# First attention of a perceiver block: the key and value projection split over four steps, its row tiles moved behind p * v, its evictions in every second step

## The chip, the cores and the metric

The kernel runs on one core of one Trainium2 chip. The metric is the device time of one execution in microseconds (us); several executions of the same kernel are listed and their median is used. All data are f32.

## The reference

The program is six residual blocks in a row, on 128 queries of width 256. The change is in the first one, a cross attention from the queries to a context of 12544 rows of width 192, with 16 heads of width 16:

```python
x = x + L0_xattn(layernorm(x), ctx)      # the changed part
x = x + L0_attn(layernorm(x)); x = x + L0_ffn(layernorm(x))
x = x + L1_xattn(layernorm(x), ctx); x = x + L1_attn(layernorm(x)); x = x + L1_ffn(layernorm(x))

def L0_xattn(x, y):                      # y: 12544 x 192
    q = x @ Wq + bq; k = y @ Wk + bk; v = y @ Wv + bv       # 16 heads of 16
    attn = softmax(q k^T / sqrt(16))                        # per head, 128 x 12544
    out = attn v
    return relu(out @ W1 + b1) @ W2 + b2
```

## The kernel before, in words

The first attention goes over the context twice, for eight heads (an octet, 128 columns of k and v) at a time. The context is cut into superblocks of 1024 rows; a pass has twelve full ones and a last one of 256 rows. Each superblock gives four groups of 256 rows (the last one gives one), so there are 98 groups in all.

One step t of the loop issues, by hand (the order is written out, nothing reorders it), on each engine's queue:

- TensorE (PE): the scores of group t (L428, eight matmuls as four row tiles of 32), at times the transposes for a range maximum, then the pieces of the projection for group t + 4 (AHEAD = 4), then p * v of group t - 13 (LAG = 13; L530, in four column tiles of 32), then at times more transposes. Where the flag `same` is true, the pieces of the projection come behind p * v instead of ahead of it.
- ScalarE (ACT): two copies of the scores from PSUM to SBUF (L441), then two exponents of group t - 12 (L517).
- VectorE (DVE): two running maxima over the scores (L447; they read the same PSUM tiles as the two copies, in the other order), one part of the shift by the maximum (L506), then the evictions of the projection from PSUM: keys with bias (L390), values (L256).
- GpSimd (POOL): the larger part of the shift by the maximum for group t - 12 (L506).

The scores of a step take two PSUM tiles of two banks each, and there are only these: the scores of step t + 1 use the banks of step t. The projection and the small transposes share two banks with the tag "w"; two more banks are single ("m", "o").

The projection of one superblock is made of a key unit and a value unit. A unit has *row tiles* (`tiled`, the 64 rest rows of the 192, for both halves r of the superblock at once, in row tiles of 64; L209 for keys, L227 for values) and two *whole* parts (`whole(r)`, the 128 main rows for one half; L212, L234), then one eviction for each half (`keys_out`, `values_out`). With g the number of a group in its superblock, the pieces in step t are those of group t + 4: g = 0 key row tiles, whole(0) and eviction 0; g = 1 key whole(1) and eviction 1; g = 2 and 3 the same for the values. An *even* step below is one whose pieces have g 0 or 2, an *odd* step one with g 1 or 3.

Groups are taken in ranges of ten (or nine), each with its own maximum. The first step of a range, called step +0 here, also folds the maximum of the range before it (L464 or L462, DVE), transposes it on PE (L474) and reduces it on DVE (L475). Step +1 spreads it out with transposes on PE (L250) and two copies on ACT (L494). A range's p * v ends two steps after the next range but one has begun: in step +2 its result is copied (L540), in step +3 turned by two transposes on PE into a "w" bank (`gather`, L245) and stored (L546). In the second pass one such gather falls on step +4.

While t is under 12, the evictions are on ACT, after that on DVE. In the steps up to 13 there is no p * v.

Of the kernel before, what the change touches and what calls it, by code (L numbers as in the profile page):

```python
# [13 lines left out]
P = 128  # L14
# [19 lines left out]
def perceiver(ctx: ExitStack, tc: tile.TileContext, a: dict, out: bass.AP):  # L34
    nc = tc.nc
# [5 lines left out]
    banks = {}  # L41
# [34 lines left out]
    def context_weight(pool, name, ap):  # L76
# [18 lines left out]
        out=headmask, in_=headmask, compare_op=ALU.is_ge, fill=0.0, base=0,  # L95
# [3 lines left out]
        out=headmask, in_=headmask, compare_op=ALU.is_ge, fill=0.0, base=15,  # L99
# [4 lines left out]
    for u in range(2):  # L104
# [6 lines left out]
        out=causal, in_=causal, compare_op=ALU.is_ge, fill=-1e10, base=0,  # L111
# [71 lines left out]
    NS = (SK + SB - 1) // SB  # L183
# [32 lines left out]
    def project_values(name, wv, cx, j, bank=None):  # L216

        lo, hi, h = cx
        ps = [(bank or ps_w)(f"{name}_{r}") for r in range(2)]
        js = slice(j * P, (j + 1) * P)  # L220

        def tiled():
            for kc in range(h // P):
                ks = slice(kc * P, (kc + 1) * P)
                for r in range(2):
                    rs = slice(64 * r, 64 * r + 64)
                    nc.tensor.matmul(  # L227
                        ps[r][:, ks], hi[rs, ks], wv[1][rs, js], start=(kc == 0), stop=False,
                        skip_group_check=True,
                    )  # L230

        def whole(r):
            for kc in range(h // P):
                nc.tensor.matmul(  # L234
                    ps[r][:, kc * P : (kc + 1) * P], lo[:, r * h + kc * P : r * h + (kc + 1) * P],
                    wv[0][:, js], start=False, stop=True, skip_group_check=True,
                )

        return ps, tiled, whole
# [59 lines left out]
    with tc.tile_pool(name="l0w", bufs=1) as lw:  # L299
# [8 lines left out]
        with tc.tile_pool(name="l0x", bufs=1) as work, ExitStack() as ps0:  # L308
# [51 lines left out]
            def spare(name):  # L360

                return bank_o(name) if name.endswith("_1") else bank_m(name)

            def behind(t):

                return ((1, 2), (3, 4), (5, 6), (7,))[t] if t < 4 else (t + AHEAD,)

            def pieces(t):

                if t >= len(groups):  # L370
                    return []
# [8 lines left out]
                work_of = {"k": ([], [], []), "v": ([], [], [])}  # L380
# [16 lines left out]
                def first_half(kind, make, w, evacuate):  # L397
                    bank = spare if kind == "v" and m < 2 else None
                    unit = make(f"x0_{kind}{m}", w, ctxs[m], j, bank)
                    tiled, whole, out = work_of[kind]  # L400
                    tiled.append(unit[1])
                    whole.append(lambda: unit[2](0))
                    out.append(lambda: evacuate(0, unit[0][0]))
                    deferred[m, kind] = lambda: unit[2](1), lambda: evacuate(1, unit[0][1])
# [5 lines left out]
                short = s == NS - 1  # L410
                if g == 0:
                    first_half("k", project_keys, xwk, keys_out)
                if g == 1 or short:
                    second_half("k")
                if g == 2 or short:
                    first_half("v", project_values, xwv, values_out)
                if g == 3 or short:
                    second_half("v")
                return [f for kind in "kv" for part in work_of[kind] for f in part]

            def scores(t):
                m, g = groups[t]
# [126 lines left out]
                )  # L549

            with tc.manual_schedule():
                tiled, whole, k_out = pieces(0)
                tiled()
                whole()
                early = ps_s("x0_early")
                _, xnT = layernorm(x, "ln0", early[:, 0])
                k_out()
                queries(0, xnT, early[:, 1])
                oTs = {}

                spread_at = {max(l + 2, l0 + LAG - 2): b for b, (l0, l) in enumerate(zip(start_of, last_of))}
                for t in range(len(groups) + LAG + 1):
                    e, o = t - LAG + 1, t - LAG
                    e = e if 0 <= e < len(groups) else None
                    o = o if 0 <= o < len(groups) else None
                    st = scores(t) if t < len(groups) else None
                    ended = range_of[t - 1] if 1 <= t < len(groups) + 1 and last[t - 1] else None
                    b = spread_at.get(t)
                    spread = range_spread(b) if b is not None else None
                    if e is not None:  # L570
                        shifted_gpsimd(e)
                        if first[e]:
                            shifted_vector(e)
# [739 lines left out]
```

## Time and profile before

| | us |
|---|---|
| median of 3 runs | 1596.38 |
| lowest, highest | 1593.13, 1598.63 |
| the profiled execution's own time | 1592.66 |
| its span | 1590.9 |
| first scores of the first attention start at | 13.86 |
| step +1 of its last but one range: spread maximum copied, by | 402.3 |
| last exponents of the first attention end at about | 456 |

The granted clock of TensorE was 0.987 of full speed over the span and 1.00 in the stretch from 0 to 440 us. A profile comes from one execution; its rows give, for groups of equal instructions, the count, the busy time, the mean duration of one, and the idle time of the engine ahead of them with the instruction that ended it. A timeline row gives the start, the length, the engine, the line and the operation, and in brackets the idle time ahead and what ended it. Each f32 matmul shows as two records of it. A chain of waits tells which instruction each one waited for last.

### The profile page before, as it was taken

To read this page: it belongs to the slowest core of one execution; us is meant where nothing else is said; L and a number is where in the kernel's file an instruction comes from. 1 tells how busy PE (TensorE), PEld (TensorE's weight loads), DVE (VectorE), ACT (ScalarE), POOL (GpSimd) and SP (SyncE) were. 2 spreads that over 40 slices of the span, in tenths; PEclk is the share of its full clock that TensorE was granted. 3 is DMA by queue.
4 is the path that set the end of the run, shared out by engine and by line. 5 is a ranking of instruction groups with operands and counts; after the bars stand their busy time and mean duration, and the time that the engine had idled before them with its cause. 6 is when DMAs were issued, how large, how long until landed. Compare 5 with 4: busy or idle time off the path is not lost.

```text
span 1590.9 us, 39751 instructions
## 1 busy us (share of the span) xinstructions
PE 1507.9 (95%) x17130; PEld 1156.8 (73%) x17130; DVE 1169.4 (74%) x1238; ACT 996.3 (63%) x1221; POOL 851.1 (54%) x559
## 2 busy tenths in 40 slices
PE   7999989999789998999999999999999999999978
PEld 4566666666545877877778787787787777777868
DVE  4798978999863327677777777777777777778952
ACT  5898979889853225665655665565665655655531
POOL 0588877888820000863863864864764764761000
PEclk9999999999997999999999999999999999999979
DMA  3211112111193661322222222232232222225930
GB/s 104 61 41 42 46 42 61 41 42 46 47 270 129 238 167 25 98 84 83 83 80 86 81 81 86 80 93 74 87 94 80 87 81 86 81 81 153 306 135 4
DMA packets 68737, 146.62 MB, mean 92 GB/s; under 512 B 8905, under 2 KB 27089, under 8 KB 68562
## 3 DMA queue, kind: packets, MB, share of 16 engines
q1 hardware_dynamic: 68258, 143.30, 30.0%
q8 instruction: 135, 2.21, 0.6%
q10 hardware_dynamic: 304, 0.79, 0.2%
q14 instruction: 40, 0.33, 0.1%
HBM read 143.92 MB, written 0.13 MB: 91 GB/s over the span
## 4 chain that ended last, share of the span: by engine, by line
PE 62%; DVE 6%; ACT 2%; POOL 1%; DMA 1%; issue 1%; SPq 0%; DVEq 0%; ACTq 0%
PE x_s L958 11%; PE x_v L234 10%; PE x_o L1043 10%; PE x_k L212 9%; PE x_v L227 5%; PE x_k L209 4%; PE f_h L1249 2%; PE f_h L824 2%; PE k L212 2%; PE f_py L841 2%; DVE x_part L1066 1%; POOL x_p L506 1%; PE k L209 1%; DVE x_folded L1005 1%; PE f_py L1258 1%
## 5 line engine op out<-in xcount | busy, mean ns | idle before, releaser
L1024 POOL TENSOR_TENSOR x_p<-x_p,x_spread 128x1024 f32<-128x1024 f32 (+1 forms) x175 | 402.6, 2324 | 165.1 <-ACT x_spread L1017 164.9
L506 POOL TENSOR_TENSOR x_p<-x_p,x_spread 128x512 f32<-128x512 f32 (+1 forms) x184 | 325.6, 1820 | 121.0 <-ACT x_spread L494 61.1
L1066 DVE TENSOR_REDUCE x_part<-x_p 128x256 f32<-128x1024 f32 (+1 forms) x175 | 329.4, 1923 | 1.6 <-ACT x_p L1032 1.6
L975 ACT COPY x_p<-x_s 128x1024 f32<-128x1024 f32 (+1 forms) x200 | 198.0, 996 | 177.7 <-DVE x_mx L982 97.9
L982 DVE TENSOR_TENSOR x_mx<-x_s,x_mx 128x1024 f32<-128x1024 f32 (+1 forms) x161 | 193.4, 1201 | 127.1 <-PE x_s L958 118.7
L1071 POOL TENSOR_TENSOR x_sums<-x_sums,x_part 128x256 f32<-128x256 f32 x161 | 118.7, 738 | 303.4 <-DVE x_part L1066 303.1
L441 ACT COPY x_p<-x_s 128x1024 f32<-128x1024 f32 x196 | 193.4, 1016 | 48.5 <-PE x_s L428 33.2
L234 PEld LDWEIGHTS x_v<-ywv_lo,x_ctx_lo 128*128 128x128 f32 x1568 | 189.3, 192 | 38.3 <-issue 36.8
L1032 ACT ACTIVATE x_p<-x_p 128x1024 f32<-128x1024 f32 (+1 forms) x200 | 197.8, 1037 | 1.4 <-DVE x_p L1024 1.3
L517 ACT ACTIVATE x_p<-x_p 128x1024 f32<-128x1024 f32 x196 | 196.3, 1062 | 0.2 <-DVE x_p L506 0.2
L1043 PE MATMUL x_o<-x_p,x_v 128*64 128x128 f32 x3136 | 193.6, 276 | 0.4
L234 PE MATMUL x_v<-ywv_lo,x_ctx_lo 128*128 128x128 f32 x1568 | 193.1, 276 | 0.0
L447 DVE TENSOR_TENSOR x_mx<-x_s,x_mx 128x1024 f32<-128x1024 f32 x140 | 168.2, 1221 | 32.1 <-PE x_s L428 17.2
L1043 PEld LDWEIGHTS x_o<-x_p,x_v 128*64 128x64 f32 x3136 | 169.6, 137 | 12.3 <-issue 1.5
L958 PE MATMUL x_s<-x_qT,x_kT 64*128 64x128 f32 x2744 | 177.7, 279 | 0.0
L212 PE MATMUL x_k<-x_ctx_lo,ywk_lo 128*128 128x512 f32 (+1 forms) x364 | 171.6, 594 | 0.0
L958 PEld LDWEIGHTS x_s<-x_qT,x_kT 64*128 64x128 f32 x2744 | 160.2, 188 | 15.6 <-issue 15.4
L943 ACT COPY x_v<-x_v 128x512 f32<-128x512 f32 (+1 forms) x208 | 116.2, 563 | 79.3 <-PE x_v L234 78.8
L227 PEld LDWEIGHTS x_v<-ywv_hi,x_ctx_hi 64*128 64x128 f32 x1568 | 106.8, 188 | 48.4 <-issue 25.1
L428 PE MATMUL x_s<-x_qz,x_kT 32*128 32x256 f32 x1568 | 117.6, 401 | 17.7 <-ACT x_p L441 16.6
L530 PE MATMUL x_o<-x_p,x_v 128*32 128x128 f32 x3136 | 111.7, 276 | 10.0 <-ACT x_p L517 8.5
L530 PEld LDWEIGHTS x_o<-x_p,x_v 128*32 128x32 f32 x3136 | 81.9, 109 | 53.9 <-ACT x_p L517 18.9
(257 smaller groups left out, 1761.1 us busy)
## 6 DMA issues: line engine op xcount, KB each, us to landing
x_ctx_lo<-in_ctxT_dram SPq DMA_DIRECT2D x119, 512.0 KB, 4.0
x_ctx_hi<-in_ctxT_dram SPq DMA_DIRECT2D x238, 128.0 KB, 3.8
f_w<-in_L_ffn_W_dram SPq DMA_DIRECT2D x32, 512.0 KB, 4.9
k_lo<-in_ctxT_dram SPq DMA_DIRECT2D x12, 512.0 KB, 10.0
f_gating<-n_kernel_gating_EDF_dram SPq DMA_DIRECT2D x8, 512.0 KB, 6.9
f_up<-L_ffn_kernel_up_EDF_dram SPq DMA_DIRECT2D x8, 512.0 KB, 7.5
f_wd<-ffn_kernel_down_EFD_dram SPq DMA_DIRECT2D x8, 512.0 KB, 7.3
k_hi<-in_ctxT_dram SPq DMA_DIRECT2D x24, 128.0 KB, 7.9
```

The costliest lines, as they stand in the source:

```text
L212: nc.tensor.matmul(ps[r][:, :h], wk[0][:, js], lo[:, r * h : (r + 1) * h], start=False, stop=True)
L234: nc.tensor.matmul(ps[r][:, kc * P : (kc + 1) * P], lo[:, r * h + kc * P : r * h + (kc + 1) * P], wv[0][:, js], start=False, stop=True, sk ...
L441: nc.scalar.copy(ps[t][k], st[k].rearrange("p a n -> p (a n)"))
L506: engine.tensor_tensor(v, v, by[:, banks].unsqueeze(2).to_broadcast([P, n, 2, 256]), ALU.add)
L517: nc.scalar.activation(ps[t][k], ps[t][k], AF.Exp)
L530: nc.tensor.matmul(os[b][32 * i : 32 * i + 32, u * P : (u + 1) * P], v[:, 2 * g + c, 17 * (2 * i + u) : 17 * (2 * i + u) + 32], p[i // 2][ ...
L958: nc.tensor.matmul(st[:, u, c * P : (c + 1) * P], kTs[t][rs, ks], qT[rs, j, :], start=True, stop=True)
L975: nc.scalar.copy(scores_kept(ps[t][i], sts[i].shape[2] // P), sts[i])
L1024: engine.tensor_tensor(v, v, spreads[j].unsqueeze(2).to_broadcast([P, 2, n, P]), ALU.add)
L1032: nc.scalar.activation(v, v, AF.Exp)
L1043: nc.tensor.matmul(o[us, 0:P], vs[t][:, c0 + c, us], p[:, n0 : n0 + P], start=(c0 + c == 0), stop=(c0 + c == total - 1), skip_group_check= ...
L1066: nc.vector.tensor_reduce(part, v, AX.X, ALU.add)
```

## The change

Only the first attention is changed. A key or value unit now has its first whole part cut in two (`of=2`). An even step issues the row tiles and the first half of whole(0), and no eviction; the odd step after it issues the second half of whole(0), eviction 0, whole(1) and eviction 1. The key row tiles are cut in two with the rest, 256 columns each where they were 512. In even steps the pieces are now issued behind p * v; in odd steps they are ahead of it, as before. Where an even step also needs a "w" bank for a range maximum, a spread or a gather (`shared`), the old cut stays: row tiles, whole(0) and eviction 0 in the even step. The short last superblock stays whole, key unit and then value unit. The first pieces are issued in another grouping to match (`left`).

```diff
-    def project_keys(name, wk, cx, j, bank=None):
+    def project_keys(name, wk, cx, j, bank=None, of=1):
...
         def tiled():
-            for r in range(2):
-                rs = slice(64 * r, 64 * r + 64)
-                nc.tensor.matmul(ps[r][:, :h], wk[1][rs, js], hi[rs, :h], start=True, stop=False)
-
-        def whole(r):
-            nc.tensor.matmul(ps[r][:, :h], wk[0][:, js], lo[:, r * h : (r + 1) * h], start=False, stop=True)
+            for i in range(of):
+                n = slice(i * h // of, (i + 1) * h // of)
+                for r in range(2):
+                    rs = slice(64 * r, 64 * r + 64)
+                    nc.tensor.matmul(
+                        ps[r][:, n], wk[1][rs, js], hi[rs, n], start=(i == 0), stop=False, skip_group_check=True
+                    )
+
+        def whole(r, parts=range(of)):
+            for i in parts:
+                n = h // of
+                nc.tensor.matmul(
+                    ps[r][:, i * n : (i + 1) * n], wk[0][:, js], lo[:, r * h + i * n : r * h + (i + 1) * n],
+                    start=False, stop=True, skip_group_check=True,
+                )
...
-        def whole(r):
-            for kc in range(h // P):
+        def whole(r, parts=range(of)):
+            n = h // P // of
+            for kc in range(parts.start * n, parts.stop * n):
...
+            spread_at = {max(l + 2, l0 + LAG - 2): b for b, (l0, l) in enumerate(zip(start_of, last_of))}
+
+            def shared(t):
+
+                return t > 0 and (last[t - 1] or (t > LAG and last[t - LAG - 1]) or t + 1 in spread_at)
+
             def behind(t):
 
-                return ((1, 2), (3, 4), (5, 6), (7,))[t] if t < 4 else (t + AHEAD,)
+                return ((2,), (3, 4), (5, 6), (7,))[t] if t < 4 else (t + AHEAD,)
...
+                def first_half(kind):
+                    (banks, tiled, whole), out = deferred[m, kind] = unit(kind)
+                    if shared(t - AHEAD):
+                        return [tiled, lambda: whole(0), lambda: out(0, banks[0])]
+                    return [tiled, lambda: whole(0, range(0, 1))]
 
                 def second_half(kind):
-                    for part, f in zip(work_of[kind][1:], deferred.pop((m, kind))):
-                        part.append(f)
...
+                    (banks, tiled, whole), out = deferred.pop((m, kind))
+                    rest = [lambda: whole(0, range(1, 2)), lambda: out(0, banks[0])]
+                    return (rest if not shared(t - 1 - AHEAD) else []) + [lambda: whole(1), lambda: out(1, banks[1])]
...
+                return (first_half, second_half)[g % 2]("kv"[g // 2])
...
-                tiled, whole, k_out = pieces(0)
-                tiled()
-                whole()
+                (tiled, lo0), (lo1, k_out, *left) = pieces(0), pieces(1)
+                for f in (tiled, lo0, lo1):
+                    f()
...
-                    ahead = [f for n in behind(t) for f in pieces(n)]
+                    ahead = left + [f for n in behind(t) for f in pieces(n)]
+                    left = []
...
                         (m, g), (mo, go) = groups[t + AHEAD], groups[o]
-                        short = sbs[m][1] == NS - 1
-                        same = m % NV == mo % NV and (short or g == 3 or (g == 2 and go < 2))
+                        same = g % 2 == 0 or (m % NV == mo % NV and g == 3)
                     for f in () if same else ahead:
                         f()
```

More of the change, by code (lines that the diff above doesn't have):

```diff
@@ L206, in tiled, with project_values @@
         def tiled():
-            for r in range(2):
-                rs = slice(64 * r, 64 * r + 64)
-                nc.tensor.matmul(ps[r][:, :h], wk[1][rs, js], hi[rs, :h], start=True, stop=False)
-        def whole(r):
-            nc.tensor.matmul(ps[r][:, :h], wk[0][:, js], lo[:, r * h : (r + 1) * h], start=False, stop=True)
+            for i in range(of):
[12 more added lines that the diff above has]
+                )
         return ps, tiled, whole
-    def project_values(name, wv, cx, j, bank=None):
+    def project_values(name, wv, cx, j, bank=None, of=1):
         lo, hi, h = cx
@@ L379, in pieces @@
                 bias = cols[:, COL_BK + j : COL_BK + j + 1]
-                work_of = {"k": ([], [], []), "v": ([], [], [])}
                 filling = t < LAG - 1 + AHEAD
@@ L395, in values_out @@
                     evacuated(filling, dst, src[:, :h].rearrange("p (k h d) -> p k h d", h=8, d=16))
-                def first_half(kind, make, w, evacuate):
-                    bank = spare if kind == "v" and m < 2 else None
[L399 to L404, printed above, removed]
@@ L406, in second_half @@
-                def second_half(kind):
-                    for part, f in zip(work_of[kind][1:], deferred.pop((m, kind))):
-                        part.append(f)
[L410 to L418, printed above, removed]
@@ L419, in pieces, with unit @@
-                return [f for kind in "kv" for part in work_of[kind] for f in part]
+                def unit(kind):
+                    if kind == "k":
+                        make, w, out = project_keys, xwk, keys_out
+                    else:
+                        make, w, out = project_values, xwv, values_out
+                    bank = spare if kind == "v" and m < 2 else None
+                    return make(f"x0_{kind}{m}", w, ctxs[m], j, bank, 1 if s == NS - 1 else 2), out
+                def first_half(kind):
[3 more added lines that the diff above has]
+                    return [tiled, lambda: whole(0, range(0, 1))]
@@ new lines, in second_half @@
+                def second_half(kind):
+                    (banks, tiled, whole), out = deferred.pop((m, kind))
+                    rest = [lambda: whole(0, range(1, 2)), lambda: out(0, banks[0])]
+                    return (rest if not shared(t - 1 - AHEAD) else []) + [lambda: whole(1), lambda: out(1, banks[1])]
+                if s == NS - 1:
+                    both = [unit(kind) for kind in "kv"]
+                    return [
+                        f for (banks, tiled, whole), out in both for f in (
+                            tiled, lambda whole=whole: whole(0), lambda whole=whole: whole(1),
+                            lambda out=out, banks=banks: out(0, banks[0]),
+                            lambda out=out, banks=banks: out(1, banks[1]),
+                        )
+                    ]
@@ L559, in perceiver @@
                 oTs = {}
-                spread_at = {max(l + 2, l0 + LAG - 2): b for b, (l0, l) in enumerate(zip(start_of, last_of))}
                 for t in range(len(groups) + LAG + 1):
```

## The prediction

> **What bounds the kernel now.** The page first: over the span PE looks full.
>
> ```profile
> PE 1507.9 (95%) x17130; PEld 1156.8 (73%) x17130; DVE 1169.4 (74%) x1238; ACT 996.3 (63%) x1221; POOL 851.1 (54%) x559
> ```
>
> These are averages over six blocks. The change touches only the steps of the first attention, so I read the waits between 60 and 400 us.
>
> ```profile
> ACT x_p L441 <- PE x_s L428: 22.6, 16, 2.5
> PEld x_s L428 <- ACT x_p L441: 21.8, 38, 1.1
> ...
> DVE x_mx L447 <- ACT x_p L441: 12.3, 29, 1.7
> ACT x_p L441 <- DVE x_mx L447: 12.1, 39, 0.4
> ```
>
> No engine is always the last: the copy waits for the scores, the scores for the copy, and copy and maximum for each other. That is a ring, so I take one pair of steps from the timeline (even at 167.90, odd at 172.37, next even at 175.99).
>
> ```profile
> 167.90 1.16 PE L428 MATMUL x_s<-x_qz,x_kT 32*128 32x256 f32 x16 [0.41 <-ACT x_p L441]
> ...
> 168.99 1.35 PE L227 MATMUL x_v<-xwv_hi,x_ctx_hi 64*128 64x128 f32 x16
> 169.14 1.23 DVE L447 TENSOR_TENSOR x_mx<-x_s,x_mx 128x1024 f32<-128x1024 f32 x1
> 169.65 1.92 ACT L441 COPY x_p<-x_s 128x1024 f32<-128x1024 f32 x2
> ...
> 170.27 1.16 PE L234 MATMUL x_v<-xwv_lo,x_ctx_lo 128*128 128x128 f32 x8
> 170.68 1.23 DVE L447 TENSOR_TENSOR x_mx<-x_s,x_mx 128x1024 f32<-128x1024 f32 x1 [0.32 <-ACT x_p L441]
> ...
> 171.36 1.08 PE L530 MATMUL x_o<-x_p,x_v 128*32 128x128 f32 x32
> 171.44 2.02 ACT L517 ACTIVATE x_p<-x_p 128x1024 f32<-128x1024 f32 x2
> ...
> 172.37 1.15 PE L428 MATMUL x_s<-x_qz,x_kT 32*128 32x256 f32 x16
> 172.42 0.68 DVE L256 COPY x_v<-x_v 128x512 f32<-128x512 f32 x1
> ...
> 173.60 1.01 ACT L441 COPY x_p<-x_s 128x1024 f32<-128x1024 f32 x1
> 173.61 2.36 DVE L447 TENSOR_TENSOR x_mx<-x_s,x_mx 128x1024 f32<-128x1024 f32 x2 [0.50 <-PE x_s L428]
> ...
> 174.92 1.02 ACT L441 COPY x_p<-x_s 128x1024 f32<-128x1024 f32 x1 [0.30 <-DVE x_mx L447]
> ```
>
> The even step is PE's: the starts lie 1.09 (scores), 1.28 (row tiles), 1.09 (whole), 1.01 (p * v) apart, 4.47 us, with no gap. With keys it is 4.35 (159.93 to 164.28). The odd step is the ring over the single score banks: scores to first copy 1.23, first to second copy 1.32 (0.30 of it waiting for the maximum), second copy to the next scores 1.07, 3.62 us; PE waits 0.4 of it. A pair is 8.09 (values) or 7.97 (keys).
>
> [...] 39 copies wait for the maximum, 29 maxima for the copy. [...] the maximum at 169.14 starts only when the key eviction ahead of it (168.39, 0.74 us) is through. [...] Here two key row tiles of 512 columns take 1.06 us and one whole part 1.05. [...]
>
> **The change part by part**, with starts of neighbours, not durations, as prices.
>
> PE work. No column is added. An even step becomes scores 1.08, p * v 1.01, row tiles 1.06 (keys) or 1.09 (values, the price where they did not wait; the 1.28 came from a bank that the eviction had not freed), half a whole part 0.53: 3.7. An odd step: 1.08 + 0.53 + 1.05 + 1.01 = 3.7. That takes 0.7 off PE's even step. The key unit goes from 4 to 8 matmuls, so 4 more weight loads (188 ns each on PEld). I cost them at nothing: a value whole part loads four times in 1.09 us where a key one loads once in 1.05; matmuls hide them. Loads of the context keep their place in the queue of SP, whose issues start a superblock's step as before; POOL's instructions and order stay.
>
> A new wait on PE. p * v of group t - 13 needs exponents which ACT issues at the end of step t - 1. Now, in even steps, it comes directly behind the scores. One step in the trace has that order already (213.11): its exponents end at 214.20, and the next matmuls start at 215.25, which is 1.17 after ACT came free at 214.08. Behind it stand row tiles, half a whole part and the scores. From ACT's first copy in an even step to that in the odd step this chain is 1.17 + 1.06 + 0.53 + 1.24 = 4.00. The odd one has ACT alone: 0.90 (copy) + 2.81 (second copy, two exponents; 131.84 to 134.65) = 3.71. These two would allow pairs of 7.71.
>
> The evictions. Their number stays, but both now stand in DVE's queue in the odd step, between its shift and the next even step's maxima. The first of these maxima holds up the second copy of the scores, which is ahead of the exponents. The ring over two steps: maximum to second copy 1.31; second copy to the next first copy 2.81; first copy to second maximum 1.03 (169.65 to 170.68); to the shift 1.14; to the eviction 0.60; two evictions 2 x 0.66 (keys; 133.39 to 134.05) or 2 x 0.60 (values; 176.48 to 177.08); then the maximum. Sum 8.21 or 8.09. With one eviction the same ring is 7.55, under today's pair, which is why it doesn't show before. So two pairs take 16.30 against 16.06 today: **+0.12 us per pair**, although PE is shorter. About two free pairs in each of 8 ranges: +2.0.
>
> Fold at step +0. It starts when DVE has finished the odd step: 3.48 us after the first copy now (173.60 to 177.08), later 1.03 + 1.14 + 0.60 + 1.20 to 1.32 = 3.97 to 4.09. PE is done earlier than the transposes of the maximum, which wait for DVE, so this passes on whole: 8 folds (steps 20 to 89) x 0.5 = +4.0.
>
> Gather at step +3. Its two transposes go to a "w" bank. Before, that bank's eviction was in the even step, and they started behind p * v (150.95). Now the built program has them wait for the first of the two evictions: 1.14 + 1.14 + 0.60 = 2.88 us after the first copy, the bank free 0.73 later (138.05 to 138.78), transposes 0.37, next scores, copy 1.24: 5.22 us from first copy to first copy, 4.20 before (149.19 to 153.39): +1.0. The step before it gains the exponent wait, +0.3: ACT is late there (free at 145.48), so scores come at 145.48 + 1.17 + 1.06 + 0.53 = 148.24 for 147.57, the copy at 149.48 for 149.19. Gathers in steps 23, 33, 43, 62, 72, 82: 6 x 1.3 = +7.8. The gather of step 53 is in an even, shared step: only +0.3.
>
> The start. Step 0 has half a whole part less (-0.5). Steps 4 to 10 are the ring of scores and copies (3.17 per step), which covers the rest.
>
> The end. From 402.1 us POOL runs 17 shifts back to back for 32 us, and the next fold waits behind them; what is late after step 90 is hidden there, so the gather of step 92 counts nothing.
>
> Sum: 2.0 + 4.0 + 7.8 + 0.3 - 0.5 = **+13.6 us**. On the profiled execution's own time, 1592.66, that is 1606.3. The median shown is 3.7 higher, which would give 1610.0. I take 1608.
>
> Unknowns. A maximum that is 0.38 late, as the ring gives it, is not in the trace (longest such wait of the copy 0.4 with 0.1 late): 0 to 0.8 per pair. The weight loads: 0 to 18 (below). Value row tiles behind p * v: 1.09 to 1.28; over the 24 full value units up to 4.6 more, if they were on the path. A gain beyond PE's slack is excluded by the ACT price, 3.71 a step.
>
> **The rivals.**
>
> A. The balance pays: the late maximum costs less, because DVE catches up in the even step, which has no eviction, and the gather fits in. Then pairs are 7.71 for 8.02: some 20 pairs in free steps, -6; if the steps around the gathers gain as well, 77 steps x 0.15 = -12. 1580 to 1590. For it: the odd step now has no PE wait and the maximum comes early there. Against: the built program's order on DVE, both evictions ahead of the maximum. It decides if the two evictions together cost under about 0.8 us, for then the ring is under 7.71; the rows say 1.2 to 1.3.
>
> B. The weight loads are not hidden: 24 full key units x 4 x 0.188 = 18 us more, 1626. Against: the value rows.
>
> C. No change: the waits of the gather are taken from PE's saved 0.7 and leave within 0.3% (about 5 us, what a measurement of this kernel can tell). 1592 to 1601. That the change doesn't do what it says is excluded: the built program has the new order on PE and DVE.
>
> **How the numbers follow.** Forecast 0.65, A 0.20, B 0.05, C 0.10. The forecast's own range is 1601 to 1618: between half the gathers' cost and 8 us more. For 8 in 10 it goes down to the upper end of A, 1588, and up to 1619. Faster 0.20, same 0.11 (C and a little of the forecast), slower 0.69.
>
> **What would show it.** Right: in the free pairs a copy L441 (new line number) that waits 0.6 to 0.8 for DVE in every even step, no PE row tiles right behind scores, pairs of 8.1 to 8.2; two transposes of the gather ended by an eviction; ranges of ten steps near 44.5 to 45 us for 43. Wrong: pairs under 7.9, or gather transposes right behind p * v; then A. Key whole parts above 0.56 for 256 columns: B.

## The result, and the profile after

The changed kernel takes **1606.84 us** in the median of 7 runs (1603.44 to 1613.92), the kernel before 1596.38 (1593.05 to 1598.63, 7 runs). The ratio is **1.0084, 95% interval 1.0064 to 1.0103**: slower by 0.8%, some 13 us; the two medians differ by 10.5. The profiled span is 1605.0 us, against 1590.9.

PE's line of the page shows 192 more records, which is 96 more f32 matmuls (each shows as two). PEld, the weight loads, is busy 32.7 us longer. DVE is busy 12.3 us less with the same 1238 instructions; where that comes from shows at the folds below.

```profile
PE 1516.5 (94%) x17322; PEld 1189.5 (74%) x17322; DVE 1157.1 (72%) x1238; ACT 996.3 (62%) x1221; POOL 850.8 (53%) x559
```

Some waits of the kernel after between 60 and 412 us (total, how often, longest):

```profile
...
DVE x_mx L471 <- PE x_s L452: 40.0, 50, 2.0
ACT x_p L465 <- PE x_s L452: 28.5, 23, 3.5
PEld x_o L554 <- ACT x_p L541: 28.0, 57, 0.8
ACT x_p L465 <- DVE x_mx L471: 16.3, 43, 0.7
...
PEld x_s L452 <- ACT x_p L465: 11.1, 34, 1.1
PE x_o L554 <- ACT x_p L541: 10.0, 31, 0.5
...
PEld x_ot L255 <- DVE x_kT L405: 5.8, 4, 1.5
```

The wait of the scores for the copy has halved (22.4 before in the same stretch, now 11.1). In its place the weights of p * v (L554) wait 28.0 us for the exponents (L541; 5.3 before), and the gather's transposes (L255) wait 5.8 for an eviction (L405; 0.8 before). The timeline shows where, in the pair that the prediction took (steps 38 and 39, now at 173.89 and 178.51, next even step at 182.14):

```profile
173.89 1.34 PE L452 MATMUL x_s<-x_qz,x_kT 32*128 32x256 f32 x16
...
174.55 1.40 DVE L405 TENSOR_SCALAR x_kT<-x_k,cols 128x512 f32<-128x512 f32 x2
...
175.16 0.41 PE L554 MATMUL x_o<-x_p,x_v 128*32 128x128 f32 x4
175.63 1.01 ACT L465 COPY x_p<-x_s 128x1024 f32<-128x1024 f32 x1
...
175.78 1.07 PE L554 MATMUL x_o<-x_p,x_v 128*32 128x128 f32 x28 [0.21 <-ACT x_p L541]
175.88 2.34 DVE L471 TENSOR_TENSOR x_mx<-x_s,x_mx 128x1024 f32<-128x1024 f32 x2
176.78 1.16 PE L236 MATMUL x_v<-xwv_hi,x_ctx_hi 64*128 64x128 f32 x16
177.18 1.01 ACT L465 COPY x_p<-x_s 128x1024 f32<-128x1024 f32 x1 [0.54 <-DVE x_mx L471]
177.87 0.71 PE L244 MATMUL x_v<-xwv_lo,x_ctx_lo 128*128 128x128 f32 x4
...
178.51 1.15 PE L452 MATMUL x_s<-x_qz,x_kT 32*128 32x256 f32 x16
...
179.75 2.50 DVE L471 TENSOR_TENSOR x_mx<-x_s,x_mx 128x1024 f32<-128x1024 f32 x2 [0.94 <-PE x_s L452]
...
181.07 1.02 ACT L465 COPY x_p<-x_s 128x1024 f32<-128x1024 f32 x1
...
182.14 1.30 PE L452 MATMUL x_s<-x_qz,x_kT 32*128 32x256 f32 x16
...
182.76 1.28 DVE L266 COPY x_v<-x_v 128x512 f32<-128x512 f32 x2
...
184.03 1.07 PE L554 MATMUL x_o<-x_p,x_v 128*32 128x128 f32 x28 [0.26 <-ACT x_p L541]
```

The even step has half the whole part (177.87) and is still longer, 4.62 us for 4.47: p * v spreads over 1.62 us (175.16 to 176.78) because its later matmuls wait for the second exponent. The two evictions stand together (174.55), the next maximum starts at 175.88, and the second copy waits 0.54 for it. In the odd step the maximum (179.75) waits for the scores, and the second copy (181.07) comes when this maximum is through.

Two tables hold all runs together. First the steps, by the distance of the starts of scores:

| | before | after | difference |
|---|---|---|---|
| pair, keys / values | 7.97 / 8.09 | 8.22 / 8.25 | +0.25 / +0.16 |
| steps +2, +3, +4 around a gather (t = 32 to 34) | 4.20, 4.07, 4.67 | 4.97, 5.28, 3.8 to 3.9 | +1.2 for the three |
| step +0 (fold), sum of 8 | | | +2.5 |
| step 12 to step 90 | 340.75 | 353.15 | +12.4 |

The second measure is POOL's: its shifts of a full range of ten run back to back, so the distance from the first shift of one range to that of the next is the length of a range. Before, then after:

```profile
100.61 35.77 POOL L506 TENSOR_TENSOR x_p<-x_p,x_spread 128x1024 f32<-128x1024 f32 x20 [7.19 <-ACT x_spread L494]
143.56 35.76 POOL L506 TENSOR_TENSOR x_p<-x_p,x_spread 128x1024 f32<-128x1024 f32 x20 [7.19 <-DVE x_mx L447]
```

```profile
103.34 35.74 POOL L530 TENSOR_TENSOR x_p<-x_p,x_spread 128x1024 f32<-128x1024 f32 x20 [7.92 <-ACT x_spread L518]
147.99 35.76 POOL L530 TENSOR_TENSOR x_p<-x_p,x_spread 128x1024 f32<-128x1024 f32 x20 [8.91 <-DVE x_mx L471]
```

The columns are start, length, engine, line, instruction, and in brackets the idle time ahead. A range took 42.95 us (143.56 - 100.61) and takes 44.65. POOL's own 35.8 us are unchanged; its pause, from the last shift over the folds to the next spread maximum, grew from 7.2 to 8.9.

### The profile page after: what moved, and what is told of

Same layout as the page of the kernel before. It is cut to its first block, busy times and chain, and to the rows that moved or that the text cites. A ratio compares the mean times of both kernels' runs of the same rounds, so it can differ in the third digit from the quotient of the medians.

```text
span 1605.0 us, 40150 instructions
## 1 busy us (share of the span) xinstructions
PE 1516.5 (94%) x17322; PEld 1189.5 (74%) x17322; DVE 1157.1 (72%) x1238; ACT 996.3 (62%) x1221; POOL 850.8 (53%) x559
## 4 chain that ended last, share of the span: by engine, by line
PE 71%; DVE 14%; ACT 11%; issue 3%; DMA 1%; SPq 0%; DVEq 0%; ACTq 0%
PE x_s L981 11%; PE x_v L244 11%; PE x_k L218 11%; PE x_o L1066 9%; PE x_v L236 6%; PE x_k L211 5%; ACT x_p L541 5%; ACT x_p L465 4%; PE x_s L452 4%; DVE x_mx L471 4%; PE x_o L554 2%; PE f_h L1272 2%; PE f_h L847 2%; PE f_py L864 2%; PE k L218 2%
## 5 line engine op out<-in xcount | busy, mean ns | idle before, releaser
L541 ACT ACTIVATE x_p<-x_p 128x1024 f32<-128x1024 f32 x196 | 196.0, 1059 | 0.2 <-DVE x_p L530 0.2
L1066 PEld LDWEIGHTS x_o<-x_p,x_v 128*64 128x64 f32 x3136 | 169.7, 137 | 12.4 <-issue 1.7
L554 PE MATMUL x_o<-x_p,x_v 128*32 128x128 f32 x3136 | 125.6, 279 | 20.0 <-ACT x_p L541 18.5
L554 PEld LDWEIGHTS x_o<-x_p,x_v 128*32 128x32 f32 x3136 | 87.1, 110 | 60.3 <-ACT x_p L541 43.0
```

The lines of the kernel that those rows point to most:

```text
L541: nc.scalar.activation(ps[t][k], ps[t][k], AF.Exp)
L554: nc.tensor.matmul(os[b][32 * i : 32 * i + 32, u * P : (u + 1) * P], v[:, 2 * g + c, 17 * (2 * i + u) : 17 * (2 * i + u) + 32], p[i // 2][ ...
L1066: nc.tensor.matmul(o[us, 0:P], vs[t][:, c0 + c, us], p[:, n0 : n0 + P], start=(c0 + c == 0), stop=(c0 + c == total - 1), skip_group_check= ...
```

## The experiments

Theory 1 is the prediction's: the two evictions in a row on DVE set the pair. Theory 2: p * v directly behind the scores waits for exponents, and this chain through PE and ACT sets the pair. Ratios are to the kernel before, run on the same chip beside each.

| kernel | median us | before us | ratio (95%) | pairs, keys / values (t = 36, 38) | range |
|---|---|---|---|---|---|
| after | 1606.84 | 1596.38 | 1.0084 (1.0064 to 1.0103) | 8.22 / 8.25 | 44.65 |
| e1_order | 1606.22 | 1594.70 | 1.0071 (1.0045 to 1.0098) | 8.46 / 8.30 | 44.03 |
| e2_split | 1615.48 | 1594.70 | 1.0134 (1.0110 to 1.0159) | 8.64 / 8.70 | 45.64 |
| e3_gather | 1601.74 | 1594.70 | 1.0049 (1.0030 to 1.0069) | 8.21 / 8.25 | 44.33 |
| e4b_more | 1617.00 | 1592.93 | 1.0141 (1.0109 to 1.0172) | 8.55 / 8.72 | 45.42 |
| e5_control | 1612.16 | 1592.93 | 1.0111 (1.0082 to 1.0140) | 8.20 / 8.26 | 44.69 |
| e5_lag | 1626.92 | 1592.93 | 1.0202 (1.0177 to 1.0227) | 7.63 / 8.01 | 43.98 |
| e6_lag_split | 1623.51 | 1592.93 | 1.0191 (1.0158 to 1.0223) | 7.85 / 7.90 | 43.30 |
| e7_evict_first | 1594.42 | 1595.19 | 0.9992 (0.9982 to 1.0002) | 7.84 / 7.90 | 42.94 |
| e9_pool | 1594.88 | 1594.77 | 0.9999 (0.9988 to 1.0011) | 7.97 / 8.09 | 42.10 |
| e8_pool_evict | 1587.15 | 1594.77 | **0.9948 (0.9933 to 0.9963)** | 7.84 / 8.02 | 41.73 |

(Range: the second to the third of POOL's rows, as above.)

### e1_order: the new split, pieces ahead of p * v

```diff
-                        same = g % 2 == 0 or (m % NV == mo % NV and g == 3)
+                        same = m % NV == mo % NV and g == 3
```

> The changed kernel with the pieces of even steps ahead of p * v again; the split and the evictions stay as changed. Theory 1 (on record in the prediction: the two evictions in a row make the next step's first maximum late, and that ring sets the pair): pairs of free steps stay at 8.1 to 8.2, the time at 1604 to 1609. Theory 2 (p * v directly behind the scores waits for the exponents of the step before, and what stands behind it makes the next scores late): that wait goes, pairs fall to about 7.9 unless the row tiles now wait for the two evictions instead, which would hold them near 8.1; time 1599 to 1604.

Measured: 1.0071, not told apart from after's 1.0084. The wait for exponents is gone and another one is there. Waits of e1_order, 60 to 412 us:

```profile
PEld x_v L236 <- DVE x_kT L405: 12.3, 23, 2.5
```

The row tiles, now right behind the scores, wait for the bank that the second eviction has not freed; pairs of 8.14 to 8.55, with one of 7.74 (steps 57 and 58). So the order alone neither made the loss nor would have saved it: with both evictions late, the row tiles have to stand behind something.

### e2_split: the old split, still behind p * v

```diff
-                    if shared(t - AHEAD):
+                    if True:
                         return [tiled, lambda: whole(0), lambda: out(0, banks[0])]
...
-                    return (rest if not shared(t - 1 - AHEAD) else []) + [lambda: whole(1), lambda: out(1, banks[1])]
+                    return [lambda: whole(1), lambda: out(1, banks[1])]
...
```

(The part left out groups the first pieces as before.)

> The changed kernel with the old split everywhere (row tiles, the whole of whole(0) and eviction 0 in the even step, whole(1) and eviction 1 in the odd one), still behind p * v in even steps. Theory 1: one eviction per step again, no late maximum, no gather behind an eviction: pairs fall to 8.0 or below, time 1597 to 1602. Theory 2: the chain from the exponents over p * v, row tiles and whole part to the next scores gets 0.5 us longer in every even step: pairs near 8.7, some 35 of them, minus about 7 us for the gathers that no longer wait: 1612 to 1620.

Measured: 1615.48, 1.0134, pairs of 8.64 and 8.70. One even step of it, from the timeline:

```profile
169.58 1.16 PE L452 MATMUL x_s<-x_qz,x_kT 32*128 32x256 f32 x16 [0.37 <-ACT x_p L465]
...
170.67 0.41 PE L554 MATMUL x_o<-x_p,x_v 128*32 128x128 f32 x4
...
171.48 1.07 PE L554 MATMUL x_o<-x_p,x_v 128*32 128x128 f32 x28 [0.40 <-ACT x_p L541]
...
172.48 1.13 PE L211 MATMUL x_k<-x_ctx_hi,xwk_hi 64*128 64x256 f32 x8
...
173.54 1.13 PE L218 MATMUL x_k<-x_ctx_lo,xwk_lo 128*128 128x256 f32 x4
174.60 1.15 PE L452 MATMUL x_s<-x_qz,x_kT 32*128 32x256 f32 x16
174.71 0.75 DVE L405 TENSOR_SCALAR x_kT<-x_k,cols 128x512 f32<-128x512 f32 x1 [0.53 <-PE x_k L218]
```

DVE waits here, it is not waited for: the evictions stand apart, one of them idles 0.53 for PE. The step is 1.09 (scores), 1.81 (p * v, which took 1.01 in the odd step), 1.06, 1.06: 5.02. The pair does not fall with the evictions apart, as theory 1 alone had it; theory 2's chain sets the pair of this kernel. How near the evictions' ring is in the kernel after, e2_split can't tell, since it makes the other chain longer. Half a whole part more (0.53) made the pair 0.42 to 0.45 longer, so in the kernel after the exponent chain had 0.1 to spare at most. What this run also says: the move behind p * v, with each eviction back in its old step, costs more than the whole change does (1.0134 and 1.0084, intervals apart); moving half a whole part and an eviction to the odd step pays part of it back.

### e4_more and e4b_more: a third eviction of half the width

```diff
-                    ... + [lambda: whole(1), lambda: out(1, banks[1])]
+                    ... + [lambda: whole(1), lambda: out(1, banks[1]), lambda: again(kind, banks[1])]
```

`again` copies 256 columns of the same bank once more to the place where they already are. In e4_more the key copy went, by a slip, into the value tile, which changes the output: 1615.33 us, 1.0131, pairs of 8.54 and 8.53.

> The changed kernel with a third, half as wide eviction from the same bank behind the other two in odd steps (it writes the same values again), about 0.35 us more on DVE in each of some 35 pairs. Theory 1 (the evictions' ring sets the pair): all of it shows, 10 to 13 us more, 1617 to 1620. Theory 2 (the exponents' ring sets it and the evictions have some 0.2 us to spare): 3 to 6 us more, 1609 to 1613.

> As e4_more, with the third, half as wide eviction now into the tile of its own unit (in e4_more that of a key unit went into the value tile, so p * v of other values was computed and waits on that tile came in). About 0.35 us more on DVE in each of some 35 pairs. Theory 1 (evictions' ring): pairs 8.5 to 8.55, 10 to 13 us over the changed kernel. Theory 2 (exponents' ring alone, evictions with 0.2 us to spare): pairs near 8.35, 3 to 6 us over it. Both rings near one length: in between.

Measured (e4b_more): 1617.00, pairs of 8.55 and 8.72. The extra instruction takes 0.48 us, and these lines of its timeline show it arriving on the path:

```profile
178.69 0.48 DVE L415 TENSOR_SCALAR x_kT<-x_k,cols 128x256 f32<-128x256 f32 x1
...
180.40 1.01 ACT L473 COPY x_p<-x_s 128x1024 f32<-128x1024 f32 x1 [1.19 <-DVE x_mx L479]
```

From the first eviction to the maximum it is now 1.84 us (177.25 to 179.09), 1.33 in the kernel after. From evictions to the next pair's evictions it is 8.73 us with keys and 8.54 with values, where the kernel after has 8.21 and 8.08: theory 1's ring took the addition whole. The pairs, taken by the scores, grew by 0.33 and 0.47. Neither theory alone gives that with e2_split. Both rings have nearly one length: lengthen either, and the pair grows by almost all of it.

### e5_control, e5_lag, e6_lag_split: p * v one step later

e5_lag gives p * v fourteen steps of lag, so its exponents are a step old. It holds one more set of score tiles; what is given up for it (one spread tile, and one key tile with a small one for the short superblock in its place) is given up in e5_control too. To keep the key tiles apart, e5_lag also holds back some evictions.

```diff
...
-                for t in range(len(groups) + LAG + 1):
-                    e, o = t - LAG + 1, t - LAG
+                for t in range(len(groups) + LAG + 2):
+                    e, o = t - LAG + 1, t - LAG - 1
...
```

> The changed kernel with two key tiles where there were three (a small one for the short superblock) and one tile for the spread maxima where there were two; nothing else. It is the control for e5_lag, which needs the room. Expected by both theories: within 1 us per range of the changed kernel, 1604 to 1613, pairs of free steps unchanged at 8.2.

> e5_control with p * v one step later (group t - 14; exponents stay at t - 12), so that its exponents are long done when it follows the scores. The evictions stay two in a row, the gather falls on step +4. Theory 1 (evictions' ring, which stays): free pairs 8.1 to 8.2 as before this edit; only the gathers gain (6 x 1): 3 to 7 us under e5_control. Theory 2 (the exponents' wait sets the pair): free pairs fall to 7.7 to 8.0, in all 9 to 16 us under e5_control.

Measured: e5_control leaves the pairs alone and loses 3 us in step 49 (10.13 us, 7.37 in after), where fewer tiles are free. In e5_lag the pairs fall, to 7.63 with keys and to 8.01 with values, about what theory 2 forecast. The total went the other way, 1626.92 us: steps 49, 53, 57 and 61, with my held evictions, take 16.1, 9.0, 9.0 and 8.6 us, and a gather's step 6.7 to 7.3. So its total says nothing on the theories, and its pairs say less than they seem to. The gather's step (here step 34) has the old cut and takes one eviction early, so only one is left in front of the maximum of the next pair, the one of 7.63. The pair at 173.89 has both:

```profile
174.50 1.40 DVE L407 TENSOR_SCALAR x_kT<-x_k,cols 128x512 f32<-128x512 f32 x2
...
182.71 1.28 DVE L266 COPY x_v<-x_v 128x512 f32<-128x512 f32 x2
```

From evictions to evictions that is 8.21 us, just what the prediction had summed for theory 1's ring (with values in front it is 8.09, also as summed). PE shows no wait for an exponent here, and the second copy waits 0.48 for the maximum. The scores lie only 8.01 apart because the shorter pair ahead had left room: they start 0.61 before the evictions at the beginning (173.89) and 0.81 at the end (181.90). So with the exponents' wait gone, theory 1's ring is still there at its full length.

> e5_lag with the old split (one eviction per step, whole(0) in the even step), row tiles behind p * v. Neither the exponents nor two evictions stand in the way: even step 1.08 + 1.01 + 1.06 to 1.09 + 1.05 to 1.09 = 4.2 to 4.3, odd step 3.62: pairs of 7.8 to 7.9, which is 0.15 to 0.2 under the kernel before; 1585 to 1595 if the smaller key and spread room costs little. If the order of row tiles behind p * v costs by itself, pairs stay at 8.2 or above.

Measured (e6_lag_split, the old split on top, as in e2_split): pairs of 7.85 and 7.90, below those of the kernel before, so with older exponents row tiles behind p * v are no loss, but a small gain. The total, 1623.51, has e5_lag's side costs (step 49: 15.5 us).

### e3_gather: the old cut in the step ahead of a gather

```diff
-                return t > 0 and (last[t - 1] or (t > LAG and last[t - LAG - 1]) or t + 1 in spread_at)
+                return t > 0 and (last[t - 1] or (t > LAG and last[t - LAG - 1]) or (t >= LAG and last[t - LAG]) or t + 1 in spread_at)
```

> The changed kernel with the old cut also in step +2 of each range, so that the bank of the gather in step +3 is free before. Both theories: step +3 falls from 5.2 to about 4.1 us, step +2 grows by up to 0.5, step +4 gives back up to 0.8 of what it had gained: net 2 to 5 us less than the changed kernel, 1602 to 1605. Rival (the gather's wait was hidden by the steps around it): no difference, 1606 to 1608.

Measured: 1601.74, 1.0049 (1.0030 to 1.0069) against 1.0084: 5.6 us of the loss is back by the ratios, though the intervals overlap; in the profiles step 12 to step 96 takes 378.02 us for 381.26. Step +3 falls from 5.2 to 3.62 and its transposes no longer wait; but step +2 is 5.41 to 5.49, since it has the whole part and the exponent wait again. This is how the gather looked in the kernel after:

```profile
156.89 1.40 DVE L405 TENSOR_SCALAR x_kT<-x_k,cols 128x512 f32<-128x512 f32 x2
157.69 0.20 PEld L255 LDWEIGHTS x_ot<-ident,x_oT 128*128 128x128 f32 x2 [1.52 <-DVE x_kT L405]
157.69 0.44 PE L255 MATMUL x_ot<-ident,x_oT 128*128 128x128 f32 x2 [1.26 <-DVE x_kT L405]
...
158.06 1.15 PE L452 MATMUL x_s<-x_qz,x_kT 32*128 32x256 f32 x16
```

and in e3_gather:

```profile
155.72 0.44 PE L255 MATMUL x_ot<-ident,x_oT 128*128 128x128 f32 x2
...
156.18 1.17 PE L452 MATMUL x_s<-x_qz,x_kT 32*128 32x256 f32 x16
156.67 0.74 DVE L405 TENSOR_SCALAR x_kT<-x_k,cols 128x512 f32<-128x512 f32 x1
```

### e7_evict_first: could faster pairs have paid at all?

The kernel before, with DVE's shift behind the eviction in steps without the end of a range, so that PE's bank comes free 0.6 us earlier.

```diff
-                    if 0 <= t - LAG + 2 < len(groups) and not first[t - LAG + 2]:
+                    if (ended is not None) and 0 <= t - LAG + 2 < len(groups) and not first[t - LAG + 2]:
                         shifted_vector(t - LAG + 2)
...
+                    if (ended is None) and 0 <= t - LAG + 2 < len(groups) and not first[t - LAG + 2]:
+                        shifted_vector(t - LAG + 2)
```

> The kernel before, with one edit: in steps without a range end, DVE's shift comes behind the eviction instead of ahead of it. In the kernel before, the row tiles behind the scores take 1.28 (values) or 1.18 us (keys) and not 1.09 or 1.06, because the eviction that frees their second bank is behind the shift. If that is the cause, the eviction ends 0.6 us earlier, the row tiles take 1.06 to 1.09, free pairs fall from 7.97 and 8.09 to 7.82 to 7.9, some 35 pairs: 3 to 6 us under the kernel before, 1587 to 1592. If the eviction then waits for its whole part on PE and keeps the shift back, or the row tiles' 1.28 has another cause: no difference, 1591 to 1597.

Measured: the row tiles behind the scores take 1.06 us (keys, 165.34) and 1.09 (values, 173.18) where they took 1.18 and 1.28 (161.03 and 168.99 in the kernel before); the pairs fell to 7.84 and 7.90, and nothing came of it: 0.9992. A range is 42.94 us, as before. POOL tells why:

```profile
147.87 2.38 POOL L506 TENSOR_TENSOR x_p<-x_p,x_spread 128x1024 f32<-128x1024 f32 x1 [7.18 <-DVE x_mx L447]
```

Its pause is 7.18 us again, and its 35.8 us of shifts are what they were. The pair of fold instructions in the same range, in the kernel before, in e7_evict_first and in the kernel after (start, length of both together):

```profile
134.05 3.48 DVE L464 TENSOR_TENSOR x_spread<-x_mx 128x512 f32<-128x512 f32 x2
```

```profile
138.06 3.79 DVE L464 TENSOR_TENSOR x_spread<-x_mx 128x512 f32<-128x512 f32 x2
```

```profile
139.18 1.28 DVE L488 TENSOR_TENSOR x_spread<-x_mx 128x512 f32<-128x512 f32 x2
```

Two folds need 1.28 us. Before, the first of them took 2.88, and in e7_evict_first 3.19. Both were held until POOL was through with its last shift (136.38 in the kernel before, 140.7 in e7_evict_first), and ended 0.55 us after it; where no POOL shift ran, in the kernel before at 264.68, the first fold took 0.68. The fold has two SBUF inputs. DVE's shift, with one input in PSUM, shows no hold in any of 81 cases, 73 of them while a POOL shift ran; nor does the fold of a range of nine groups, which is a reduction with one SBUF input and ran beside POOL's shifts, though the last of the four only for its first 0.01 us (minimum, median and longest in ns, kernel before):

```profile
L506 DVE TENSOR_TENSOR x_p<-x_p,x_m x81: 674/678/697, 60.8 to 410.0; 128x512 f32<-128x512 f32 x81
...
L462 DVE TENSOR_REDUCE x_spread<-x_mx x4: 1232/1238/1245, 217.8 to 434.1; 128x512 f32<-128x1024 f32 x4
```

The hold outlasts one shift. POOL's last two shifts meet at 135.1 in the kernel before and at 139.4 in e7_evict_first, with the fold already begun, and it was held over that point to the end of the second one. It is so in all six held folds of the kernel before: they take 2.45 to 2.91 us and end 0.54 to 0.56 after the second shift. Why the fold is held and the other two are not, no run shows.

So in the kernel before POOL's chain bounds a range of ten steps: 35.8 us of shifts, then 7.2 us from the last shift over folds, transposes, reduction and spread to the next first shift, 43.0 in all. In e7_evict_first, with faster steps, the fold only waits longer.

### e9_pool and e8_pool_evict: POOL's chain shortened

Both start from the kernel before. In e9_pool POOL gives two of its twenty shifts to DVE; e8_pool_evict has e7_evict_first's edit as well.

```diff
             def shares(t):
...
+                if t - start_of[range_of[t]] in (3, 7):
+                    return 2, 0
...
```

> The kernel before with one edit: at the range positions 3 and 7 of the ten groups, GpSimd gives its second row of shifts to VectorE, so GpSimd has 18 shifts in a full range where it had 20, and VectorE's shift in those two groups covers 1024 columns (1.21 us) instead of 512 (0.68 us). Theory A: GpSimd's chain (20 shifts in 35.8 us and 7.2 us from the last one over the folds to the next range's spread, 43.0 us for ten steps) bounds a range of the kernel before. Then the first fold no longer runs beside a shift and takes about 0.7 us instead of 2.8, the step in which the folds stand shrinks from 6.4 - 6.5 us by up to 1 us, and VectorE's extra 1 us per range is hidden or costs at most half of that: 4 to 8 us less in all, ratio 0.995 to 0.9975. Theory B: VectorE and the ring of copies and maxima bound a range and GpSimd has slack: the two longer shifts push the next maxima by up to 0.5 us each, nothing comes back at the fold, and the time is 0 to 8 us more, ratio 1.000 to 1.005.

> The kernel before with both edits: VectorE's shift stands behind the eviction in steps without the end of a range (as in e7_evict_first, where the pairs fell to 7.84 / 7.90 us and the gain was given back at the folds), and GpSimd gives the second row of shifts to VectorE at range positions 3 and 7. Theory A (GpSimd's chain bounds the range): with the chain 3 us shorter the gain of the pairs is kept, 5 to 10 us less than before, ratio 0.9935 to 0.997. Theory B (the ring bounds the range, and e7's gain was lost for another reason): within 0.2% of before, or slower by VectorE's extra 1 us per range, ratio 0.998 to 1.005.

Measured: in both the fold takes 1.28 us. POOL in e8_pool_evict:

```profile
103.47 33.26 POOL L508 TENSOR_TENSOR x_p<-x_p,x_spread 128x1024 f32<-128x1024 f32 x18 [8.42 <-ACT x_spread L494]
145.20 33.28 POOL L508 TENSOR_TENSOR x_p<-x_p,x_spread 128x1024 f32<-128x1024 f32 x18 [8.46 <-DVE x_mx L447]
```

A range is 41.73 us for 42.95, and the whole is 0.9948 (0.9933 to 0.9963): **7.6 us faster than before on the same chip** (5 executions against 19). The gain lies in the first attention: in the profiles its scores of step 1 to its last exponents take 433.5 us for 440.7. With POOL relieved, the gain of the pairs is kept. e9_pool's total, 0.9999, missed what I expected of theory A. Its six full ranges do shrink, by 0.7 to 1.0 us each, the two around the change of pass grow by 1.1, and from the first range's first shift to that of the last range but one it takes 341.2 us for 344.4. But in the profiled execution steps 93 to 95 take 16.7 us for 13.6. There PE waited 1.42 us for an eviction behind the longer shift (1.21 us at 413.18), and then had half the granted clock for 10.2 us; the scores in it took 2.09 and 2.11 us. Whether its other executions lose the time at the same place, no run shows.

## Why the prediction was right, point by point

**Sign and size.** Forecast 1608, measured 1606.84; the sum said +13.6 us. The interval of the ratio gives 10 to 16, the medians 10.5, the profiled spans 14.1.

**Gathers: right.** Forecast 1.3 each; steps +2 to +4 together cost 1.13 to 1.24 in five of six; the third, with the step behind it, 1.17. Together 7.1 us for 7.8. The parts don't fall as forecast: in steps 32 to 34 they are +0.77, +1.21 and -0.78, where +0.3, +1.0 and nothing were summed, so the sum is good in part by luck. The transposes wait for the first eviction, as worked out (1.26 us at 157.69), and e3_gather took this wait away.

**Pairs: the size nearly right, the named ring right, a second one dismissed.** Forecast 8.21 and 8.09, measured 8.22 and 8.25; with the further +0.6 of step 48, some 3.6 us where 2.0 was forecast. The evictions' ring is in the trace as summed: from evictions to evictions 8.20 to 8.21 us with keys (174.55 to 182.76) and 8.08 to 8.09 with values (166.47 to 174.55), in 14 of the 15 pairs that have both evictions in front. But the scores lie further apart. The step that failed is "The odd one has ACT alone: 0.90 (copy) + 2.81 = 3.71. These two would allow pairs of 7.71". In the odd step the second copy also waits for its maximum, and this one for the scores: 1.24 us from scores to maximum (178.51 to 179.75) and 1.32 from there to the second copy (181.07), where 1.24 + 0.90 was summed. The even part is 4.12 (175.63 to 179.75) where 4.00 was summed. So the exponents' ring is 4.12 + 1.32 + 2.81 = 8.25, and the trace has it: from one wait of p * v to the next 8.25 (175.78 to 184.03), or 8.21 with key row tiles. That is on average 0.08 more than the evictions' ring, and the pairs of scores have its length. So a ring that I had named and then dismissed as short enough runs beside the one that I had forecast. e2_split lengthens the one, e4b_more the other, and both times the pair grows.

**Folds: the step that was over-sized.** Forecast 8 x 0.5; measured 2.5 in all (0.02 to 1.01 each). The later start, 139.18 for 134.05 in the third range, was costed in full. But the fold of the kernel before spent 2.2 us of its 3.48 waiting for POOL, and the later one starts after POOL's end and takes 1.28. I had seen 3.48 us where two of 0.68 stand and not asked why.

**Start: forecast -0.5, in these profiles +2.0 at step 12.** No part of the change explains it. The scores of step 0, after and then before:

```profile
15.43 2.09 PE L452 MATMUL x_s<-x_qz,x_kT 32*128 32x256 f32 x16 [1.05 <-DVE x_qz L362]
```

```profile
13.86 1.15 PE L428 MATMUL x_s<-x_qz,x_kT 32*128 32x256 f32 x16 [1.05 <-DVE x_qz L352]
```

PE begins later and at about half speed, 2.09 us for 1.15. So it does in e7_evict_first and e8_pool_evict (2.09 at 15.27 and at 15.39), whose step 0 is that of the kernel before. In the traces of all thirteen kernels there are two kinds of start, and what decides between them no run shows: in five the records of the granted clock begin at 11.1 to 12.2 us (11.7 in the kernel before), and these scores take 1.14 to 1.57 us; in eight they begin at 19.3 to 21.6 (19.6 in the kernel after), and the scores take 2.09. Of these eight, the four whose first pieces are grouped as in the kernel before reach step 12 at 60.9 to 61.5 us, the four with the grouping of the kernel after at 58.9 to 59.7. So where the records begin equally late, the changed kernel is 1.2 to 2.7 us earlier at step 12; the +2.0 belongs to these two executions.

**The sum.** The gather of step 53 was put at +0.3; steps 51 to 53 together came to -0.85, and why stays open. So the terms were off by +2.5 (start), +1.6 (pairs), -1.5 (folds), -1.2 (step 53) and -0.7 (gathers). The sum at step 90, 14.4 for 13.6, is better than its parts, and that is luck: without the start, which differs by execution, steps 12 to 90 took 12.4 us more where 14.1 was summed.

**The tail: wrong, and it doesn't show in the total.** The step was "what is late after step 90 is hidden there, so the gather of step 92 counts nothing". The kernel after was 14.4 us late at step 90, 16.7 at step 97 and 16.9 at the end of the last exponents (475.75 for 458.86). The gather of step 92 cost 2.3 us (steps 91 to 94), and POOL's last pause shows them, before and after:

```profile
439.14 11.21 POOL L506 TENSOR_TENSOR x_p<-x_p,x_spread 128x512 f32<-128x512 f32 x9 [5.00 <-PE x_mb L250]
```

```profile
456.02 11.22 POOL L530 TENSOR_TENSOR x_p<-x_p,x_spread 128x512 f32<-128x512 f32 x9 [7.53 <-PE x_mb L260]
```

The fold of this range did not wait for POOL's shifts: before, it started at 432.96 while they ran to 434.13, and took 1.25 us. That the spans differ by only 14.1 is due to the rest of the program, which the change doesn't touch: from the last exponents to the end it took 1132.0 us before and 1129.2 after, and for instance 1126.2 in e7_evict_first and 1133.4 in e9_pool. From the scores of step 1 to the last exponents, without the start of step 0 and without that rest, it is 440.7 us before and 454.5 after, +13.8: near the sum of +13.6, since the errors of its terms cancel.

**The rivals.** A needed the eviction ring under 7.71. It was 8.08 and 8.21. And had it been shorter, POOL's chain would probably have eaten the gain, as it did in e7_evict_first with pairs of 7.84 (not run on the changed kernel); the prediction had no such bound in it. B is refuted: the halves of the key whole parts have 256 columns, and six of their records take 1.56 us, three matmuls at 0.52, half of what 512 columns cost (1.06 in the kernel before, 162.21 to 163.27). Its price was too low as well: a matmul shows as two records, so there are 24 x 8 more loads, not 24 x 4, and PEld is busy 32.7 us longer, not 18. It does not show on PE: the half part of an even step takes 0.63 with keys (169.63 to 170.26) and 0.64 with values, whose loads are as many as before. C didn't come: PE's saved 0.5 in the even step went into p * v's wait, not into the gather.

## What to carry to other kernels

Before a step is made shorter, look for the engine whose instructions run back to back over many steps and compare the length of that period with its own work plus the pause that depends on it; here POOL's 35.8 + 7.2 us set 43.0 us. Faster steps alone gained nothing (e7_evict_first, 0.9992), a shorter chain alone nothing in the total (e9_pool, 0.9999), both together did (e8_pool_evict, 0.9948). When work is moved out of the way of one wait, measure how old the operands of the instruction are that moves up: p * v with exponents of the step just ended cost 0.8 us (1.81 for 1.01 in e2_split), with exponents one step older nothing (1.01 in e5_lag). And an instruction that takes longer than its shape does elsewhere in the trace (2.88 us beside 0.68) can be a wait that no list of waits shows.

## What the runs showed of the hardware that I had not expected

- A VectorE maximum from SBUF to SBUF (128x512, 0.68 us) took 2.88 and 3.19 us while GpSimd's shifts ran; in the trace it is busy time, not idle, and it lasted over the border between two of POOL's shifts, to 0.55 us after the second. VectorE's shift of the same size, with an operand in PSUM, was never held (81 times, 674 to 697 ns), nor was a reduction with one SBUF input (1232 to 1245 ns).
- TensorE at about half speed: 2.09 us for scores of 1.15 at the start, in the eight traces whose clock records begin at 19.3 to 21.6 us. For the time before its first record a view of the profile reads 1.00 (the kernel after, 14 to 17 us, with its first record at 19.6), which is no measurement, so the duration has to be read. And once in the middle: in e9_pool the records show half the clock from 415.0 us for 10.2 us, after a wait of 1.42 us.
